# One core, the end of a fused layer: the last product is taken in another order, into one bank for each chunk of tokens

## The chip, the core and the metric

The kernel runs on one NeuronCore of a Trainium2 chip. The metric is device time in microseconds for one execution of the whole program. Engines are named as in the profile: PE is TensorE (PEld its weight loads), DVE is VectorE, ACT is ScalarE, POOL is GpSimd, SP is SyncE, which issues nearly all the DMAs here.

## The reference

Input `x` is 2 x 1024 tokens of 512 float32 values. It is normalised, goes through linear attention with 16 heads and, beside it, through a feed-forward block with routed low-rank experts; both results are added to `x`.

```python
xn = _layernorm(x)
# attention: Q, K after elu + 1; out = (Q @ KV) / (Q . K_sum) @ wo.T + bo
# feed-forward
gate = xn @ W_gate + _lora(xn, sA_gate, sB_gate) + _expert_lora(xn, A_gate, B_gate, w)
up   = xn @ W_up   + _lora(xn, sA_up, sB_up)     + _expert_lora(xn, A_up, B_up, w)
hidden = silu(gate) * up                                       # 1376 features
ffn = hidden @ W_down + _lora(hidden, sA_down, sB_down) + _expert_lora(hidden, A_down, B_down, w)
out = x + attention + ffn
```

Everything is float32. What the change touches is the last product alone: `hidden @ W_down`, the low-rank terms of the down projection and the attention's output product, which the kernel takes as one sum over features.

## The kernel before

**Stages.** Attention and the gate and up products come first and leave features in DRAM. The last stage, which begins after line 1590, reads the features back and multiplies them by the down weights. It works in four units `u` of 512 tokens (two groups of 256); `first_unit` does the first, `unit_of_two` the others. The last unit is `u == 3`; there `nxt` is false.

**Two levels of a fast product.** A unit's product is a 2 x 2 block product (two token groups by two halves of 256 output columns), taken with seven block products instead of eight. They are numbered `p`, and `A`, `B`, `C` and `E_` in `unit_of_two` gather them: `E_` takes `p = 3`, which is needed only in the block of group 0 and column half 1, and is the last of the unit. Each `p` is again a sum over feature blocks. For three pairs of feature blocks (`PAIRS`) the same seven-product scheme is used once more, inside the 256 tokens by 256 columns: two chunks of 128 tokens (`q` = 0, 1) by two column halves of 128 (`e` = 0, 1). These inner products are numbered `r`. The single feature block left over (`SINGLE`), the last features with the bias row (`hr`) and the low-rank term (`had`) are taken plainly, for each chunk over all 256 columns (`whole`).

**Two banks for each sum.** `X_AT` says that `r` = 1, 6, 5 and 7 lie side by side in one PSUM bank, named `px..`; these are shared by several of the four blocks of the output. `Y_AT` says that `r` = 2, 4 and 3 lie in a second bank, `py..`, each in the block it belongs to (order `(e q)`), and the plain terms are added onto the same second bank. `main` issues the products in the order 1, 2, 4, then the plain terms, then 5, 6, 7, 3.

**The way out.** `read` turns the shared bank into four blocks: ACT copies the first one (L1798), DVE makes running sums (L1799, L1800, L1801), adds them to the residual tile `xr` (L1809), then adds the second bank (L1811). In the last unit L1811 is done in two halves, one for each chunk `q`, with a store to DRAM after each (`halves=True`, `store_out` at L1617, its DMA at L1620). All matmuls of these sums are issued in `term`, so they have the line L1771; the bank's name (`pxe`, `pye` for `E_`) tells them apart. The low-rank terms are issued much earlier, by `low_rank_pair` right after the second product of the unit (L1995), so the bank `held2` of `E_` is begun there.

**Order.** The order of instructions on PE, DVE, ACT and POOL is the order in which the program writes them; each engine works through its own queue and waits for the others by semaphores. PSUM banks have tags: `E_` has `held1` and `held2`; `held3` holds `ph`, the low-rank sums, until `low_rank_weighted` (L1651) has read them.

Of the kernel before, what the change touches and what calls it, by code (L numbers as in the profile page):

```python
# [10 lines left out]
F32 = mybir.dt.float32  # L11
# [4 lines left out]
P = 128  # L16
# [21 lines left out]
def layer_kernel(  # L38
# [23 lines left out]
    nc = tc.nc  # L62
# [29 lines left out]
    NQ = UT // P  # L92
# [9 lines left out]
    def pool(stack, name, bufs=1, **k):  # L102
        return stack.enter_context(tc.tile_pool(name=name, bufs=bufs, reuse_waits="tile", **k))
# [91 lines left out]
    for b in range(NBATCH):  # L195
        t = p2.tile([P, 2, NC, 32], F32, name=f"ksd{b}")
# [41 lines left out]
    ps_pool = [pool(psum1, "ps1", space=PSUM)]  # L238
# [256 lines left out]
    class Finish:  # L495


        def __init__(self, b, pg, ksum):
            self.b, self.pg, self.ksum = b, pg, ksum
            self.made = 0  # L500
# [889 lines left out]
    B_OF = {1: 0, 2: 2, 3: 3, 4: 7, 5: 4, 6: 5, 7: 6}  # L1390
# [111 lines left out]
    feats = {}  # L1502
# [48 lines left out]
    for j in range(NP - 1):  # L1551
        if j > 0:
            load_weights(j + 1)
        first, second = next_pair(j + 1)
# [39 lines left out]
    H_OF = {1: 0, 2: 2, 3: 7, 4: 3, 5: 4, 6: 5, 7: 6}  # L1594
    ORDER = (1, 6, 5, 2, 7, 3, 4)
    d1, d2 = slice(0, HD), slice(HD, D)
    V, G = nc.vector, nc.gpsimd
# [10 lines left out]
    xq = {}  # L1608

    def load_out(u, g, h):  # L1610
        b, s = divmod(u, 2)
        first = b * BT + g * TB + s * UT
        t = p4w.tile([P, NQ, HD], F32, tag=f"xr{g}{h}", name=f"xr{u}_{g}{h}")
        nc.sync.dma_start(out=t, in_=x[first : first + UT, h * HD : (h + 1) * HD].rearrange("(q p) d -> p q d", p=P))
        xq[u, g, h] = t

    def store_out(u, g, h, q=slice(0, NQ)):  # L1617
        b, s = divmod(u, 2)
        first = b * BT + g * TB + s * UT
        nc.sync.dma_start(  # L1620
            out=out[first : first + UT, h * HD : (h + 1) * HD].rearrange("(q p) d -> p q d", p=P)[:, q, :],
            in_=xq[u, g, h][:, q, :],
        )

    def tmp(tag, name):
        return p4w.tile([P, D], F32, tag=tag, name=name, bufs=2 if tag == "w" else 1)
# [19 lines left out]
    def low_rank_weighted(u):  # L1646
        b, s = divmod(u, 2)
        had = p4w.tile([P, UT], F32, tag="had", name=f"had{u}")
        for g in range(2):
# [5 lines left out]
    LEFT = {2: (0, wdr[:, d1], bd_sb[:, d1]), 7: (1, wdr[:, d2], bd_sb[:, d2]),  # L1655
            3: (0, wdr[:, d2], bd_sb[:, d2]), 4: (1, wdr_diff, bd_diff)}

    def weights(n):
        return wd[n] if n < NP else kvo[n - NP]


    PAIRS = ((0, 1), (2, 3), (NP, NP + 1))
    SINGLE = NP - 1
    EH = HD // 2
# [5 lines left out]
    def t_at(k, i, sl):  # L1670

        if sl.start == 0:
            return weights(PAIRS[k][i // 2])[:, 1:2, (e0, e1)[i % 2]]
        return tw[k][:, i, sl.start - 2 : sl.stop - 2, :]
# [16 lines left out]
    def in_turn(*gs):  # L1691
        gs = list(gs)
        while gs:
            gs = [g for g in gs if next(g, gs) is not gs]

    def right(k, r, p):
        w0, w1 = (weights(n)[:, B_OF[p], :] for n in PAIRS[k])
        if r in (4, 5, 6):
            i = {5: 0, 6: 1, 4: 2}[r]
            return t_at(k, i, slice(B_OF[p], B_OF[p] + 1))[:, 0, :]  # L1700
        return {1: w0[:, e0], 2: w1[:, e0], 3: w1[:, e1], 7: w0[:, e1]}[r]
# [31 lines left out]
    def left_of(u, k, r, p):  # L1733
        f0, f1 = (feats[u, n][:, H_OF[p], :] for n in PAIRS[k])
        if r in (3, 5, 6, 7):
            i = next(i for i, ps in enumerate(BATCHES) if p in ps)
            j = sorted(BATCHES[i], key=H_OF.get).index(p)
            return si[u, i][k][:, {5: 0, 6: 1, 7: 2, 3: 3}[r], j, :]
        return {1: f0[:, 0:P], 2: f1[:, 0:P], 4: f1[:, P:UT]}[r]


    X_AT = {1: 0, 6: 1, 5: 2, 7: 3}
# [5 lines left out]
    class Out:  # L1748
# [12 lines left out]
        def term(self, out, lhsT, rhs, c):  # L1761
            v = (self.x, self.y)[c]
            first = v is None
            if first:
                v = self.bank(c)
                if c:
                    self.y = v
                else:
                    self.x = v
            o = v[:, out, :] if isinstance(out, int) else v.rearrange("p (e q) n -> p q e n", q=NQ)[:, out[0]]  # L1770
            nc.tensor.matmul(o, lhsT, rhs, start=first, stop=True, skip_group_check=True)  # L1771

        def whole(self, q, lhsT, rhs):

            self.term((q,), lhsT, rhs, 1)
# [15 lines left out]
                    self.whole(q, hr[:, g, ts(q, P)], w)  # L1791
            self.products(p, (5, 6, 7, 3))

        def read(self, *to, halves=False):

            w = tmp("w", f"w{self.name}_{self.made}").rearrange("p (c n) -> p c n", n=EH)
            self.made += 1
            nc.scalar.copy(w[:, 0], self.x[:, 0])  # L1798
            V.tensor_add(w[:, 1], w[:, 0], self.x[:, 1])  # L1799
            V.tensor_add(w[:, 2], w[:, 1], self.x[:, 2])  # L1800
            V.tensor_add(w[:, 1::2], w[:, 1:3], self.x[:, 3:4].to_broadcast([P, 2, EH]))  # L1801

            def by_block(t):
                return t.rearrange("p (e q) n -> p e q n", q=NQ)

            dst = [xq[self.u, g, h] for g, h in to]
            blocks = [t.rearrange("p q (e n) -> p e q n", n=EH) for t in dst]
            if len(dst) == 1:
                V.tensor_add(blocks[0], blocks[0], by_block(w))  # L1809
                for q in (slice(0, 1), slice(1, 2)) if halves else (slice(0, NQ),):  # L1810
                    V.tensor_add(blocks[0][:, :, q], blocks[0][:, :, q], by_block(self.y)[:, :, q])  # L1811
                    if halves:
                        store_out(self.u, *to[0], q)
            else:
                V.tensor_add(w, w, self.y)
                for v in blocks:
                    V.tensor_add(v, v, by_block(w))

    def low_rank_pair(had, first, second):

        for q in range(NQ):
            for p, o in (first, second):
                g, _, w = LEFT[p]
                rows = slice(g * ER, (g + 1) * ER)
                o.whole(q, had[rows, ts(q, P)], w[rows, :])

    def last_unit(u):
        return u == 3
# [15 lines left out]
    def S12(u, ns):  # L1844
        block_sum(u, 4, V.tensor_add, 1, 3, ns)
        block_sum(u, 5, V.tensor_sub, 4, 0, ns)
# [4 lines left out]
    def S4(u, ns):  # L1851
        block_sum(u, 7, V.tensor_sub, 2, 5, ns)
# [120 lines left out]
    def unit_of_two(u, hr, before):  # L1973
        nxt = not last_unit(u)
        turn = next_kvo() if u == 1 else None
        A, B, C, E_ = (
            Out(u, n, tx, ty)
            for n, tx, ty in (("a", "ab0", "ab1"), ("b", "x0", "x1"), ("c", "x0", "held0"), ("e", "held1", "held2"))
        )

        A.main(1)
        before()
        if turn:
            turn[0](slice(0, 2))
        S12(u, range(NF) if u > 1 else range(5, NF))
        low_rank_sums(u, hr, tuple(range(NP)))
        A.read((0, 0))
        had = low_rank_weighted(u)
        if nxt:
            hr_next = load_rest(u + 1)  # L1990
            load_blocks(u + 1, slice(0, 2))
        feature_pair_sums(u, 1)

        B.main(7, hr)
        low_rank_pair(had, (3, E_), (7, B))  # L1995
        if turn:
            turn[1]()
        B.read((1, 1))

        A.main(6)  # L2000
        S4(u, range(NF))
        feature_pair_sums(u, 2, (0,))
        A.read((1, 0))
        feature_pair_sums(u, 2, (1, 2))

        B.main(4, hr)
        low_rank_pair(had, (2, C), (4, B))
        if nxt:
            load_blocks(u + 1, slice(3, 4))
        if u == 2:  # L2010
            in_turn(weight_sums(2, slice(3, 4)))
        B.read((1, 0))
        store_out(u, 1, 0)
        if nxt:
            load_out(u + 1, 1, 0)

        A.main(5)
        feature_pair_sums(u, 3)
        if nxt:
            S3(u + 1, range(NF))  # L2020
        A.read((0, 1), (1, 1))
        store_out(u, 1, 1)
        if nxt:
            load_out(u + 1, 1, 1)
        if turn:
            turn[2]()

        C.main(2, hr)
        if nxt:
            load_blocks(u + 1, slice(2, 3))  # L2030
            feature_pair_sums(u + 1, 0)
        C.read((0, 0))
        store_out(u, 0, 0)
        if nxt:
            load_out(u + 1, 0, 0)
        if turn:
            turn[0](slice(2, 3))

        E_.main(3, hr)
        if turn:  # L2040
            turn[0](slice(3, 4))

        def after():
            E_.read((0, 1), halves=not nxt)
            if nxt:
                store_out(u, 0, 1)
                load_out(u + 1, 0, 1)
            if turn:
                turn[3]()

        if not nxt:
            after()
        return (hr_next, after) if nxt else None

    for g in range(2):
        for h in range(2):
# [65 lines left out]
```

## Time and profile before

| what | value |
|---|---|
| median of 3 runs | 729.91 us (728.38 to 730.34) |
| the profiled execution | 730.1 us |
| its span in the profile | 728.3 us |
| PE busy | 717.8 us (99%) |
| DVE busy | 579.8 us (80%) |
| the last unit's last product (`E_`) begins on PE | 716.42 us |
| the last matmul ends | 723.0 us |
| the last DVE add ends | 725.35 us |

Times in the trace count from the start of the span. The profiled execution's own time is 1.8 us longer than its span: what lies around the program. PE is busy from the first slice to the last but one, so the time is the work of PE, and then a tail in which PE has nothing to do. A busy entry of PE counts one issued pass; each float32 matmul here is two passes in the records, so three products of one `r` are six records.

### The profile page before, as it was taken

The page shows a single profiled execution, that of the slowest core. Times are in us where ns is not written, and L with a number is a line of the kernel's source. Part 1 is how long each engine was busy: PE and PEld are TensorE (multiplying, and loading weights), DVE is VectorE, ACT ScalarE, POOL GpSimd, SP SyncE. Part 2 cuts the span into 40 slices and gives each one's busy share as a digit, 9 for nine tenths or more (in the row PEclk, how much of TensorE's full clock was granted, in tenths as well). Part 3 has the DMA queues.
Part 4 walks back from the last instruction along what each step waited for, and adds up shares of the span by engine and source line. Part 5 has one row for each costly group of instructions (what it writes and reads, how often), then busy time and mean ns, then how long its engine had stood idle before and what let it go on. Part 6 is the DMA issues. An engine that isn't in the chain of part 4 may idle for free.

```text
span 728.3 us, 9908 instructions
## 1 busy us (share of the span) xinstructions
PE 717.8 (99%) x3428; PEld 493.1 (68%) x3428; DVE 579.8 (80%) x1330; ACT 198.1 (27%) x438; POOL 143.4 (20%) x176
## 2 busy tenths in 40 slices
PE   8999999999999999999999999999999999999997
PEld 6666676454433566666667667566688899899896
DVE  5788767777587588878878878878988789998874
ACT  3533412454443233333333333333200000000000
POOL 4014011101000770310310310544520100000000
PEclk9999999999999999999999999999999999999999
DMA  4253000313575101211201201333662444523101
GB/s 155 85 157 106 11 1 1 97 32 112 158 212 154 26 5 58 87 32 59 88 29 59 87 30 59 116 126 134 202 195 101 134 158 132 158 87 109 59 16 44
DMA packets 61734, 66.85 MB, mean 92 GB/s; under 512 B 10866, under 2 KB 49522, under 8 KB 61428
## 3 DMA queue, kind: packets, MB, share of 16 engines
q1 hardware_dynamic: 61154, 66.20, 29.0%
q8 instruction: 27, 0.44, 0.3%
q14 instruction: 23, 0.19, 0.1%
q10 hardware_dynamic: 530, 0.02, 0.0%
HBM read 44.11 MB, written 22.09 MB: 91 GB/s over the span
## 4 chain that ended last, share of the span: by engine, by line
PE 83%; DVE 12%; ACT 3%; issue 1%; DMA 0%; DVEq 0%; ACTq 0%
PE ab L1202 16%; PE b L1262 8%; PE po L1899 7%; PE pg L401 5%; PE pya L1771 4%; PE pxa L1771 3%; PE pqu L772 3%; PE pyb L1771 3%; PE ph L1639 3%; PE x L1202 3%; PE pxb L1771 2%; PE pyc L1771 2%; PE pxa L851 2%; PE b L1257 2%; PE pr L1090 2%; PE pye L1771 2%
## 5 line engine op out<-in xcount | busy, mean ns | idle before, releaser
L1262 PE MATMUL b<-t,w 128*128 128x512 f32 x160 | 83.2, 601 | 0.7 <-DVE t L1284 0.7
L401 PE MATMUL pg<-kt,xn 128*128 128x512 f32 x128 | 58.7, 594 | 0.5 <-DVE kt L345 0.5
L1284 POOL TENSOR_TENSOR r<-r,r 128x512 f32<-128x512 f32 x20 | 30.1, 1524 | 84.5 <-DVE t L1284 82.9
L1202 PE MATMUL ab<-ti,wi 128*128 128x256 f32 x180 | 45.4, 379 | 0.0
L1202 PEld LDWEIGHTS ab<-ti,w 128*128 128x128 f32 x140 | 25.1, 189 | 29.4 <-DVE r L1230 8.2
L1284 DVE TENSOR_TENSOR r<-r,r 128x512 f32<-128x512 f32 x60 | 44.9, 788 | 0.0
L1202 PEld LDWEIGHTS ab<-ti,wi 128*128 128x128 f32 x180 | 34.2, 190 | 13.2 <-issue 5.0
L1202 PE MATMUL ab<-ti,w 128*128 128x256 f32 x140 | 41.2, 387 | 0.5 <-DVE r L1230 0.2
L401 PEld LDWEIGHTS pg<-kt,xn 128*128 128x128 f32 x128 | 23.2, 190 | 22.6 <-issue 20.6
L1235 ACT COPY r<-ab 128x256 f32<-128x256 f32 x50 | 18.6, 372 | 71.1 <-PE ab L1202 71.1
L1230 DVE TENSOR_TENSOR r<-r,ab 128x256 f32<-128x256 f32 x50 | 20.8, 417 | 20.2 <-ACT r L1227 19.7
L1262 PEld LDWEIGHTS b<-t,w 128*128 128x128 f32 x160 | 29.2, 190 | 11.3 <-issue 5.9
L1238 DVE TENSOR_TENSOR r<-r,ab 128x256 f32<-128x256 f32 x50 | 20.8, 417 | 15.9 <-ACT r L1235 15.7
L1212 ACT COPY r<-ab 128x256 f32<-128x256 f32 x50 | 18.6, 373 | 48.5 <-PE ab L1202 47.0
L1899 PE MATMUL po<-wd,f 128*128 128x256 f32 x140 | 30.9, 380 | 0.1
L410 POOL TENSOR_TENSOR ksum<-ksum,kt 128x512 f32<-128x512 f32 x12 | 15.8, 1319 | 71.7 <-DVE lg L447 42.3
L1223 ACT COPY r<-ab 128x256 f32<-128x256 f32 x50 | 18.6, 372 | 40.8 <-PE ab L1202 40.8
L1899 PEld LDWEIGHTS po<-wd,f 128*128 128x128 f32 x140 | 26.4, 190 | 4.4 <-issue 0.5
L1202 PE MATMUL ab<-xnT,w 128*128 128x256 f32 x100 | 29.4, 390 | 0.0
L1842 DVE TENSOR_TENSOR f<-f 128x256 f32<-128x256 f32 x84 | 29.3, 416 | 0.1
L1202 PE MATMUL ab<-xnT,wi 128*128 128x256 f32 x100 | 28.1, 379 | 0.0
L1202 PEld LDWEIGHTS ab<-xnT,w 128*128 128x128 f32 x100 | 18.1, 189 | 10.8 <-issue 4.5
(450 smaller groups left out, 1655.7 us busy)
## 6 DMA issues: line engine op xcount, KB each, us to landing
h_dram<-h SPq DMA_DIRECT2D x40, 256.0 KB
f<-h_dram SPq DMA_DIRECT2D x10, 512.0 KB
x_ring<-in_x_dram SPq DMA_DIRECT2D x16, 256.0 KB
q_dram<-qt SPq DMA_DIRECT2D x16, 256.0 KB
xr<-in_x_dram SPq DMA_DIRECT2D x16, 256.0 KB
out_dram<-xr SPq DMA_DIRECT2D x15, 256.0 KB
w<-in_w_up_dram SPq DMA_DIRECT2D x10, 256.0 KB
w<-in_w_gate_dram SPq DMA_DIRECT2D x10, 256.0 KB
```

The source lines that it names most:

```text
L401: nc.tensor.matmul(pg[m], xns[n][:, ts(m, P)], kt, start=(j == 0), stop=(j == TPBATCH - 1))
L772: nc.tensor.matmul(banks[c], wqs[p][:, k, ts(c, P)], tsum[b][p][:, k, :], start=(start and k == 0), stop=(k == 1), skip_group_check=True,)
L1202: nc.tensor.matmul(out, w, t, start=start, stop=True, skip_group_check=True)
L1212: nc.scalar.copy(self.r[0][:, H0], self.ua)
L1230: nc.vector.tensor_add(self.r[1][:, H1], self.r[1][:, H1], self.lo)
L1238: nc.vector.tensor_add(self.r[1][:, H0], self.r[1][:, H0], self.lo)
L1262: nc.tensor.matmul(pb[m], ws[m][:, A_OF[p], ts(k, P)], tsum[b][p][:, k, :], start=start, stop=True, skip_group_check=True)
L1284: eng.tensor_add(to[m], t[m], v[m])
L1639: nc.tensor.matmul(phs[u][g * ER : (g + 1) * ER, :], a, f[:, g, :], start=(ns[0] == 0 and n == 0), stop=(last and n == len(chunks) - 1), s ...
L1771: nc.tensor.matmul(o, lhsT, rhs, start=first, stop=True, skip_group_check=True)
L1842: op(t[:, at, :], t[:, x_, :], t[:, y, :])
L1899: nc.tensor.matmul(ps[p][:, q, :], lhsT, rhs, start=start, stop=stop, skip_group_check=True)
```

## The change

The last unit's `E_` becomes an object of a new class, `LastOut`. It computes the same sum with the same matmuls, but:

- its `finish` issues the four shared products `r` = 1, 6, 5, 7 first, into a bank `pxz` (tag `held1`), and then the instructions that turn them into blocks and add these to `xr`;
- the second bank is split: chunk 0 has a bank `pyz0` (tag `held2`), chunk 1 a bank `pyz1` (tag `held3`);
- for each chunk in turn it issues that chunk's own products (`r` = 2 and 3 for chunk 0, `r` = 4 for chunk 1), its plain terms, an add of that bank to `xr` and a store of that chunk.

The low-rank terms still come from `low_rank_pair` at the same place, now into the two banks. Units 1 and 2 are as before; `read` loses its `halves` form.

```diff
+    class LastOut:
...
+        def term(self, q, e, lhsT, rhs):
+            first = self.ys[q] is None
+            if first:
+                self.ys[q] = ps_pool[0].tile([P, 2, EH], F32, tag=f"held{2 + q}", name=f"pyz{q}")
+            nc.tensor.matmul(self.ys[q][:, e], lhsT, rhs, start=first, stop=True, skip_group_check=True)
+
+        def finish(self, p, hr, to):
+            u, w_left = self.u, LEFT[p]
+            self.x = ps_pool[0].tile([P, 4, EH], F32, tag="held1", name="pxz")
+            for r in (1, 6, 5, 7):
+                for k in range(len(PAIRS)):
+                    nc.tensor.matmul(
+                        self.x[:, X_AT[r]], left_of(u, k, r, p), right(k, r, p), start=(r == 1 and k == 0), stop=True,
+                        skip_group_check=True,
+                    )
+            w = tmp("w", "wz").rearrange("p (c n) -> p c n", n=EH)
+            t = xq[u, to[0], to[1]]
+            nc.scalar.copy(w[:, 0], self.x[:, 0])
+            V.tensor_add(w[:, 1], w[:, 0], self.x[:, 1])
+            V.tensor_add(w[:, 2], w[:, 1], self.x[:, 2])
+            V.tensor_add(w[:, 1::2], w[:, 1:3], self.x[:, 3:4].to_broadcast([P, 2, EH]))
+            by_block = w.rearrange("p (e q) n -> p q e n", q=NQ)
+            blocks = t.rearrange("p q (e n) -> p q e n", n=EH)
+            V.tensor_add(blocks, blocks, by_block)
+            f = feats[u, SINGLE][:, H_OF[p], :]
+            for q in range(NQ):
+
+                for r, e in (((2, 0), (3, 1)), ((4, 0),))[q]:
+                    for k in range(len(PAIRS)):
+                        self.term(q, slice(e, e + 1), left_of(u, k, r, p), right(k, r, p))
+                self.whole(q, f[:, ts(q, P)], weights(SINGLE)[:, B_OF[p], :])
+                self.whole(q, hr[:, w_left[0], ts(q, P)], w_left[1])
+                V.tensor_add(blocks[:, q], blocks[:, q], self.ys[q])
+                store_out(u, *to, slice(q, q + 1))
...
+        if not nxt:
+            E_ = LastOut(u)
...
+        if not nxt:
+            E_.finish(3, hr, (0, 1))
+            return None
         E_.main(3, hr)
...
         def after():
-            E_.read((0, 1), halves=not nxt)
-            if nxt:
-                store_out(u, 0, 1)
-                load_out(u + 1, 0, 1)
+            E_.read((0, 1))
+            store_out(u, 0, 1)
+            load_out(u + 1, 0, 1)
```

More of the change, by code (lines that the diff above doesn't have):

```diff
@@ L1792, in main, with read @@
             self.products(p, (5, 6, 7, 3))
-        def read(self, *to, halves=False):
+        def read(self, *to):
             w = tmp("w", f"w{self.name}_{self.made}").rearrange("p (c n) -> p c n", n=EH)
@@ L1808, in read @@
             if len(dst) == 1:
[L1809 to L1813, printed above, removed]
+                for v in (w, self.y):
+                    V.tensor_add(blocks[0], blocks[0], by_block(v))
             else:
@@ L1817, in read, with __init__, whole @@
                     V.tensor_add(v, v, by_block(w))
+    class LastOut:
+        def __init__(self, u):
+            self.u = u
+            self.x = None
+            self.ys = [None] * NQ
+        def whole(self, q, lhsT, rhs):
+            self.term(q, slice(0, 2), lhsT, rhs)
+        def term(self, q, e, lhsT, rhs):
[30 more added lines that the diff above has]
+                store_out(u, *to, slice(q, q + 1))
     def low_rank_pair(had, first, second):
@@ L2043, in after @@
         def after():
-            E_.read((0, 1), halves=not nxt)
-            if nxt:
-                store_out(u, 0, 1)
-                load_out(u + 1, 0, 1)
+            E_.read((0, 1))
+            store_out(u, 0, 1)
+            load_out(u + 1, 0, 1)
             if turn:
                 turn[3]()
-        if not nxt:
-            after()
-        return (hr_next, after) if nxt else None
+        return hr_next, after
     for g in range(2):
```

## The prediction

> **What bounds the kernel now.** I read the page's busy times first, then the chain of waits over the last microseconds, then the order of instructions on PE and DVE there, then the DMA share in narrow windows.
>
> ```profile
> PE 717.8 (99%) x3428; PEld 493.1 (68%) x3428; DVE 579.8 (80%) x1330; ACT 198.1 (27%) x438; POOL 143.4 (20%) x176
> ```
>
> PE is never idle until its last matmul ends at about 723.0 us. So only two things can move the time: less work on PE, or a shorter tail behind it. The span is 728.3 us, so that tail is 5.3 us. The chain of waits from 722 us on says what it is made of (start, length, what):
>
> ```profile
> 722.00 0.35 PE pxe L1771 x3
> 722.35 0.03 ACTq L1798
> 722.37 0.04 issue
> 722.41 0.27 ACT we L1798
> ...
> 722.71 0.30 DVE we L1799
> ...
> 723.03 0.30 DVE we L1800
> ...
> 723.35 0.43 DVE we L1801
> ...
> 723.80 0.70 DVE xr L1809
> ...
> 724.60 0.42 DVE xr L1811
> 725.02 0.33 DVEq L2118
> ```
>
> The shared bank pxe is complete at 722.33, three matmuls of r = 3 before the end of PE. Then one copy and six adds run in a row, up to 725.35: 2.35 us after the last matmul. Of these, only the last two (L1811) need the other bank. When the shared bank is filled is a matter of order, as PE's own order of time shows:
>
> ```profile
> 716.42 0.61 PE L1771 MATMUL pxe<-wd,f 128*128 128x128 f32 x4
> ...
> 718.43 1.03 PE L1771 MATMUL pye<-wd,f 128*128 128x256 f32 x4
> 719.29 1.03 PE L1771 MATMUL pye<-wdr,hr 97*128 97x256 f32 x4
> ...
> 722.61 0.39 PE L1771 MATMUL pye<-kvo,si_3b 128*128 128x128 f32 x2
> ```
>
> The reader is to see that a third of the stage (717.09 to 720.16) fills pye between two parts of pxe. The rest of the tail, 725.35 to 728.3, is the last store and the end of the program. The windows there (stretch, then PE clock, DMA share and GB/s as the last three numbers):
>
> ```profile
> 725.50:725.80 0.30, 0.00 (x0) 0.00 (x0) 0.00 (x0) 0.00 (x0) 0.00 (x0) 1.00 0.00 0
> 725.80:726.00 0.20, 0.00 (x0) 0.00 (x0) 0.00 (x0) 0.00 (x0) 0.00 (x0) 1.00 0.43 143
> 726.60:726.80 0.20, 0.00 (x0) 0.00 (x0) 0.00 (x0) 0.00 (x0) 0.00 (x0) 0.88 0.93 312
> 727.20:728.30 1.10, 0.00 (x0) 0.00 (x0) 0.00 (x0) 0.00 (x0) 0.00 (x0) 0.50 0.00 0
> ```
>
> Two stores of 128 KB start to be issued on SP at 725.05 and about 725.45. Their bytes move from about 725.85 to 726.8, and SP's wait for them (1.31 us from 725.9) ends at 727.2. The last 1.1 us is the closing of the program on all engines.
>
> [...] The trace has about 1.75 us for the last store (725.45 to 727.2), which I use.
>
> **The change, step by step.**
>
> *PE's work.* The same matmuls in another order: 21 of 128 columns and 4 of 256, besides the low-rank ones. From the timeline, three products of one r take 0.67 us (716.42 to 717.09, 720.16 to 720.83), the plain terms 0.86 us for SINGLE and 0.87 for hr, both chunks, so 0.43 each per chunk. The sum is 7 x 0.67 + 4 x 0.43 = 6.41 us, as now. Changing between the two widths costs nothing in the trace (pitches stay at 0.67 across 718.43 and 720.16). PE's end stays at 723.0. I price PE at nothing, with -0.1 to +0.3 us for the new order of banks, which the trace does not show.
>
> *The shared bank comes first.* Four r from 716.42 take 2.68 us. The last pair of records begins 0.23 us before that and lasts 0.39: complete at 719.26. The copy begins 0.08 us later, as now (722.33 to 722.41), so at 719.34. From there to the end of L1809 is 2.08 us now (722.41 to 724.49), so the blocks are in xr at 721.42. Is DVE free? Product C is read out there: its last add begins at 718.18 and lasts 0.69, so DVE is idle from 718.87 and ACT long before. This whole 2.08 us then lies beside PE's work, which goes on until 723.0: 1.58 us of cover is left. Does DVE's read of one bank slow PE's writes to another? In C's read-out it does the same (pxc read from 715.99 to 717.35 while PE fills pxe and pye), at an unchanged 0.67 us per r.
>
> *What the moved products need.* r = 6, 5, 7 are issued from 717.09 instead of 719.95. Their left sides (si) are done on DVE at 708.1, so the margin falls from 11.9 to 9.0 us: nothing. The bank held1 was last used in the unit before.
>
> *Chunk 0.* From 719.10 PE does r = 2 and 3 and two plain terms: 2 x 0.67 + 2 x 0.43 = 2.20 us, to 721.30, complete 0.16 us later (720.16 against 720.32 for such a group now): 721.46. DVE has just finished (721.42); it waits for PE and adds at about 721.54 to 721.96. SP issues the store from 722.0 to 722.4. Behind this wait on DVE's queue stands only chunk 1's add, on SP's queue only chunk 1's store, and neither could start earlier.
>
> *Chunk 1.* From 721.30: 0.67 + 2 x 0.43 = 1.53 us, to 722.83, complete at 723.0. The add begins 0.08 us later and takes 0.42: DVE ends at **723.50** instead of 725.35: **-1.85 us**. What is left behind PE is one wait and one add.
>
> *Stores.* Still two of 128 KB. Chunk 0's bytes move at about 722.85 to 723.3, before chunk 1's store is issued at 723.55; now the second issue stands behind the first one's (725.05 plus 0.37) and starts about 0.1 us after its add instead of 0.05. That is -0.05 us, with -0.3 (the last store alone on the queues, a shorter wait for its end) to +0.1 as bounds. The part from the last issue to the end, 2.85 us, stays.
>
> *The low-rank terms.* Chunk 1's now begin held3 at about 690.4, instead of the other half of held2. ph in held3 has been read when the second L1651 ends, at 684.4, and had, which the same matmul needs, comes from that instruction. No wait is new: margin 6 us. Instruction counts on every engine are equal.
>
> *Sum.* -1.85 - 0.05 = **-1.9 us**, with -2.3 to -1.5 from the bounds. Against the profiled execution: a span of 726.4 and a time of 730.1 - 1.9 = 728.2. That execution lies 0.2 us above the median of the runs, so for the median 729.91 - 1.9 = **728.0 us**, or 0.26%.
>
> **The rivals.**
>
> *As worked out, -1.9 us* (0.75). The bound of what this kernel's measurement can tell from no change is about 0.3%, 2.2 us; so the likeliest gain lies just inside it. The three runs of before spread over 1.96 us; a median taken again may fall 0.7 us to either side. So 0.45 of this case would read as over 0.3% faster.
>
> *The last store gains more, -2.2 to -2.5 us* (0.12). For it: it is alone, and the wait after its last byte (726.8 to 727.2) may shrink. Against it: C's 256 KB store, also alone, takes the same 0.85 us from issue to its first bytes, and the two last ones barely overlap now. Time about 727.6.
>
> *The wait of chunk 0's add is tied to a later matmul* (0.08). If it is released only with PE's end, both adds run from 723.08 to 723.83 and both stores follow each other as now: -1.5 us, 728.4. Against it: the banks are separate tiles, and pxe's reader is already released at 722.33, before PE's last three matmuls.
>
> *TensorE loses its pace in the new order: slower* (0.03). Between 719.3 and 722 PE would write pyz0 and pyz1 while ACT and DVE read pxz, and 128- and 256-column passes alternate more often. The gain is gone once PE's stage of 6.4 us takes 1.9 us more, and the run is measurably slower from 4.1 us, 64% more: passes of 0.11 us would have to become 0.18. At 5 us lost the time is 733. C's read-out speaks against it.
>
> *The change does nothing* (0.02): if the copy at the head of the chain still waited for PE's end, the chain would run as now, 729.9. The order on each engine is the written one, so I see no way.
>
> **How the numbers follow.** Faster by over 0.3%: 0.45 x 0.75 + 0.6 x 0.12 + 0.2 x 0.08, about 0.43. Slower: 0.03. Within: 0.54. The range: -2.3 to -1.5 us with 0.7 us of the median's own scatter on both sides gives 726.9 to 729.1, and the lower end takes in the second case. I keep that.
>
> **What would show it.** In the changed profile: PE's order pxz x24 from 716.4 to 719.1, then pyz0, then pyz1, with PE's end still at 723.0. The copy starts near 719.35, the add of the blocks ends near 721.4, the add of chunk 0 at 721.5, that of chunk 1 at 723.1 to 723.5. The chain ends PE pyz1, one DVE add. Two separate bursts of DMA, near 723 and 724.6. The span is 726.4. I am wrong if PE's stage is longer than 6.5 us, if the last add begins more than 0.2 us after PE's end, or if more than 3.0 us lie between DVE's end and the span's.

## The result, and the profile after

| | before | changed |
|---|---|---|
| median of 18 runs each | 729.94 us (726.82 to 730.58) | 726.57 us (724.57 to 728.42) |
| ratio, with its 95% interval | 1 | 0.9973 (0.9963 to 0.9983) |
| profiled execution: time, span | 730.1, 728.3 us | 724.7, 722.9 us |
| the last product begins on PE | 716.42 us | 713.15 us |
| from there to PE's end | 6.58 us | 6.59 us |
| from there to the end of the last DVE add | 8.93 us | 7.05 us |
| from there to the end of the span | 11.89 us | 9.79 us |

The ratio says 0.27% less, 2.0 us. The two medians differ by 3.4 us and the two profiled spans by 5.4 us. These are not three effects of the change. The table shows that in the profiled execution the last product already begins 3.3 us sooner, at a place in the program that the change has not reached. The stage that was changed is 2.1 us shorter. The experiments keep the two apart: from here on, times called *counted from the last product* are taken from its first matmul.

The chain of waits of the changed kernel, from 713 us on (start, length, what):

```profile
713.31 2.68 PE pxz L1838 x24
715.99 3.76 PE pyz L1831 x26
719.75 0.02 issue
719.78 0.42 DVE xr L1859
```

Where the chain of before ended in a copy and six adds behind PE, PE's own work now reaches to 719.75 and one add follows. The instructions of DVE and ACT beside it, in order of time (start, length, engine, line, operation, and in brackets the idle time before it):

```profile
716.08 0.27 ACT L1844 COPY wz<-pxz 128x128 f32<-128x128 f32 x1 [3.08 <-PE pxz L1838]
...
716.37 0.29 DVE L1845 TENSOR_TENSOR wz<-wz,pxz 128x128 f32<-128x128 f32 x1 [0.77 <-ACT wz L1844]
...
717.47 0.69 DVE L1850 TENSOR_TENSOR xr<-xr,wz 128x512 f32<-128x512 f32 x1
...
718.27 0.42 DVE L1859 TENSOR_TENSOR xr<-xr,pyz 128x256 f32<-128x256 f32 x1
...
719.78 0.42 DVE L1859 TENSOR_TENSOR xr<-xr,pyz 128x256 f32<-128x256 f32 x1 [1.09 <-PE pyz L1831]
```

The copy waits for pxz, not for PE's end: it begins at 716.08, and PE goes on to 719.75. The shared blocks are in xr at 718.16, chunk 0 is added at 718.27, and then DVE itself waits 1.09 us for PE. That last wait is the mark of a tail that has been emptied: DVE is now early. The windows of the last store (the last two numbers are the DMA share and GB/s):

```profile
721.00:721.20 0.20, 0.00 (x0) 0.00 (x0) 0.00 (x0) 0.00 (x0) 0.00 (x0) 1.00 0.52 174
721.20:721.40 0.20, 0.00 (x0) 0.00 (x0) 0.00 (x0) 0.00 (x0) 0.00 (x0) 1.00 1.05 358
721.40:721.60 0.20, 0.00 (x0) 0.00 (x0) 0.00 (x0) 0.00 (x0) 0.00 (x0) 1.00 0.39 123
721.60:723.00 1.40, 0.00 (x0) 0.00 (x0) 0.00 (x0) 0.00 (x0) 0.00 (x0) 0.83 0.00 0
```

One burst of 128 KB stands alone, where before two ran into each other for 0.95 us. The last bytes move about 1.35 us after the last add ends (720.20), against 1.45 before.

### The profile page after: what moved, and what is told of

The parts are those of the page before. It is cut to its first block, busy times and chain, and to the rows that moved or that the text cites. A ratio compares the mean times of both kernels' runs of the same rounds, so it can differ in the third digit from the quotient of the medians.

```text
span 722.9 us, 9907 instructions
## 1 busy us (share of the span) xinstructions
PE 714.9 (99%) x3428; PEld 491.3 (68%) x3428; DVE 579.9 (80%) x1330; ACT 198.2 (27%) x438; POOL 143.7 (20%) x176
## 4 chain that ended last, share of the span: by engine, by line
PE 83%; DVE 13%; ACT 3%; issue 1%; DMA 0%; DVEq 0%
PE ab L1202 16%; PE b L1262 8%; PE po L1942 7%; PE pg L401 5%; PE pya L1771 4%; PE pxa L1771 3%; PE pqu L772 3%; PE pyb L1771 3%; PE ph L1639 3%; PE x L1202 3%; PE pxb L1771 2%; PE pyc L1771 2%; PE pxa L851 2%; PE b L1257 2%; PE pr L1090 2%; PE kua L430 2%
```

## The experiments

Two theories stand against each other: the *order* theory (the tail is what must follow the bank that is filled last, so taking the shared products first is what counts) and the *banks* theory (a bank, an add and a store for each chunk bring the gain). A third question is where the 3.3 us ahead of the last product come from.

**The changed kernel again (e1_again).** No edit.

> The changed kernel once more, unaltered. Times are counted from the first matmul of the last product. Theory (the tail is shortened by the order of the products; the rest of the difference between the two profiled executions is scatter in the first 20 us): PE ends at 6.6, the last DVE add at 7.05, the span at 9.75 (each within 0.1), wherever the last product begins (713 or 716 us from the span's start). Rival (the change also makes the stages before it 3.3 us faster): the last product begins at 713 again.

The last product begins at 713.16, PE ends at 6.59, DVE at 7.04, the span at 9.79, counted from the last product. So the stage repeats. That it began at 713 again was what the rival named, and this run alone does not refute it. Two later ones do: e5, which turned out to be the same program in effect, began its last product at 714.88, and e10, the kernel before with only its start altered, at 713.11. The 18 runs gave 0.9979 (0.9969 to 0.9989), from 724.77 to 728.45 us.

**The order alone (e2_order_alone).** The shared products stay first; the chunks share one bank again, with both adds and stores at the end.

```diff
             if first:
-                self.ys[q] = ps_pool[0].tile([P, 2, EH], F32, tag=f"held{2 + q}", name=f"pyz{q}")
...
+                self.y = ps_pool[0].tile([P, NQ, 2, EH], F32, tag="held2", name="pyz")
...
-                V.tensor_add(blocks[:, q], blocks[:, q], self.ys[q])
+            for q in range(NQ):
+                V.tensor_add(blocks[:, q], blocks[:, q], self.y[:, q])
                 store_out(u, *to, slice(q, q + 1))
```

> Shared products first, but one bank for both chunks' own sums, both adds and both stores after the last matmul. Counted from the last product's first matmul. Theory (what counts is how much work waits for the bank that is filled last): PE ends at 6.6, then 0.08 of wait and both adds, 0.75: DVE ends at 7.4, the span at 10.3 with the stores close behind each other, so 1.5 us less than before. Rival (a bank, an add and a store for each chunk bring the gain): DVE ends at 8.9 and the span at 11.9, as before.

DVE's order of time at the end (PE's last matmul ends at 719.82, the last product began at 713.23):

```profile
719.86 0.75 DVE L1860 TENSOR_TENSOR xr<-xr,pyz 128x256 f32<-128x256 f32 x2 [1.62 <-PE pyz L1831]
```

Both adds now wait for PE, 1.62 us. DVE ends at 7.38 and the span at 10.34: 1.55 us of the 2.10 come from the order. That chunk 0 can be added before PE's end only from a bank of its own is not shown: no run adds it early out of a shared one. The five runs gave 0.9955 (0.9940 to 0.9970), better than the changed kernel itself. The stage cannot do that. It is a matter of the start of the program, of which more below: the runs of a kernel fall into three groups by it, and none of these five (725.36 to 727.20 us) lies in the slowest.

**The banks alone (e3_banks_alone).** A bank, an add and a store for each chunk, and the products in the old order.

```diff
...
+            shared((1,))
+            own(0, 2, 0)
+            own(1, 4, 0)
+            for q in range(NQ):
+                self.whole(q, f[:, ts(q, P)], weights(SINGLE)[:, B_OF[p], :])
+            for q in range(NQ):
+                self.whole(q, hr[:, w_left[0], ts(q, P)], w_left[1])
+            shared((6, 5, 7))
+            own(0, 3, 1)
...
```

> A bank, an add and a store for each chunk, but the products in the old order, with the shared sum complete three matmuls before the end. Counted from the last product's first matmul. Theory: as before, DVE ends at 8.9 and the span at 11.9, because the shared chain of 2.08 us still comes first and both own sums are complete long before it ends. Rival (the banks bring the gain): DVE ends at 7.1, the span at 9.8.

```profile
720.55 0.69 DVE L1866 TENSOR_TENSOR xr<-xr,wz 128x512 f32<-128x512 f32 x1
721.35 0.75 DVE L1868 TENSOR_TENSOR xr<-xr,pyz 128x256 f32<-128x256 f32 x2
```

The last product began at 713.17: DVE ends at 8.93 and the span at 11.89, the numbers of before to 0.01 us. The banks theory falls. It also speaks against a change in the stages ahead: this kernel has the changed banks and begins its last product at 713, and yet its 20 runs lie between 726.57 and 730.59 us, as those of before do (726.49 to 730.64; ratio 0.9989, 0.9978 to 0.9999).

**The shared products last (e4_shared_last).** Each chunk has its bank, add and store; its own products come first.

> Each chunk has its bank, add and store, but its own products come first and the shared products last. Counted from the last product's first matmul. Theory: the shared bank is complete at 6.6, the whole chain lies behind it: 0.08 + 2.08 + 0.11 + 0.75, DVE ends at 9.6 and the span at 12.5, 0.7 us more than before. Rival (the banks bring the gain, or any order does): at most 8.9 and 11.9.

The chain of waits at the end (PE's last matmul ends at 723.2, the last product began at 716.60):

```profile
723.26 0.27 ACT wz L1851
...
724.66 0.70 DVE xr L1857
...
725.38 0.42 DVE xr L1859
725.80 0.33 DVEq L2163
```

DVE ends at 9.53 and the span at 12.4, 0.6 and 0.5 us later than before (0.7 was expected of both; the gap ahead of the last two adds is 0.02 instead of 0.09 us, and what closes it is not shown). The same banks thus make the end faster or slower, by the order alone. The 12 runs' ratio, 1.0001 (0.9986 to 1.0016), does not show it.

**Both stores at the end (e5_stores_together).** The two stores were written after chunk 1's add.

> The changed kernel, but chunk 0's store is held back: both stores are issued after chunk 1's add. Counted from the last product's first matmul, DVE ends at 7.05 as in the changed kernel. Theory (a last store that stands alone ends the program 0.2 us sooner after its add): both stores are issued one behind the other at 7.1 and 7.5, later still than before by 0.35 us, so from DVE's end to the span's end it takes 3.1 to 3.3 us instead of 2.7 to 2.8. Rival (that part varies from execution to execution): 2.7 to 3.0 us.

The edit did not do what it was for. SP's row shows the first of the two issues at 720.45, right after chunk 0's add ended at 720.42: here SP waited for the data of the store, not for chunk 1's add, which is written ahead of it and begins at 721.50. DVE ends at 7.04 and the span at 9.79; it is in effect one more execution of the changed kernel, and the theory about the last store is not tested by it. It began its last product at 714.88.

**A longer shared chain (e6_chain_plus_2).**

```diff
...
+            spare = tmp("r", "spare").rearrange("p (c n) -> p c n", n=EH)
+            for _ in range(2):
+                V.tensor_add(spare, w, w)
             V.tensor_add(blocks, blocks, by_block)
```

> The changed kernel with two more DVE adds of 512 columns (0.69 us each, into a spare tile that nothing reads) in the shared chain, ahead of its add to xr. Counted from the last product's first matmul, the chain now ends at 5.0 and chunk 1's bank is readable at 6.6. Theory (the chain lies beside PE's work, with 1.1 us of cover besides chunk 0's add): of 1.42 us added about 0.2 to 0.3 shows: chunk 0's add begins at 6.45 instead of 5.1, DVE ends at 7.25. Rival (the chain is still on the path, or TensorE waits for it): DVE ends at 8.4 to 8.5.

```profile
719.12 1.42 DVE L1852 TENSOR_TENSOR spare<-wz 128x512 f32<-128x512 f32 x2
720.45 0.68 DVE L1853 TENSOR_TENSOR xr<-xr,wz 128x512 f32<-128x512 f32 x1
721.24 0.75 DVE L1862 TENSOR_TENSOR xr<-xr,pyz 128x256 f32<-128x256 f32 x2
```

The last product began at 714.80. Chunk 0's add begins at 6.44 and DVE ends at 7.19: of 1.42 us of work, 0.14 show. DVE no longer waits for PE at all, so the cover is used up; that further work in the chain would be paid is an estimate from this. The two stores stand close here, and from DVE's end to the span's end it takes 2.90 us instead of 2.75.

**One store (e9_one_store).** `store_out(u, *to)` once, after both adds.

> The changed kernel with one store of 256 KB after chunk 1's add in place of two of 128 KB. Counted from the last product's first matmul, DVE ends at 7.05 as in the changed kernel. Theory (what follows the last add is the last store's bytes and a fixed part): 256 KB move in 0.85 instead of 0.45 us, so from DVE's end to the span's end it takes 3.1 to 3.2 us, the span ends at 10.2. Rival (bytes don't count, only the number of stores that are close together): 2.7 to 2.8, the span at 9.8.

The last product began at 713.02, DVE ends at 7.05 (720.07), the span at 10.2 (723.2). From DVE's end to the span's end it is 3.10 us, 0.36 more than in the changed kernel. So the bytes of the last store are paid. If the first 128 KB cost as much as these further 128 KB did, the other 2.4 us don't depend on the bytes; that is an estimate from these two traces. Over all executions, one last store of 128 KB that stands alone has 2.74 to 2.75 us there (the changed kernel, e1, e5, e8), two close ones 2.90 to 2.96 (before, e2, e3, e4, e6, e10).

SP's own instructions say where the difference lies. The issues of the last two stores, in before and in the changed kernel (count, then shortest, median and longest in ns, then the starts of the first and the last):

```profile
L1620 SPq DMA_DIRECT2D out_dram<-xr x2: 345/384/424, 725.0 to 725.4; - x2
L1620 SPq DMA_DIRECT2D out_dram<-xr x2: 344/344/344, 718.7 to 720.2; - x2
```

In before the last issue stands behind the first: it begins 0.09 us after the last add and takes 0.42 us. In the changed kernel it begins 0.03 us after the add and takes 0.34. That is 0.15 us of the 0.22. The wait for the store is 0.03 us shorter (1.28 instead of 1.31), and what follows that wait 0.06 (0.98 instead of 1.04). The last part does not hang on the distance of the stores, since e4 and e6, with close ones, also have 0.98; why it varies is open.

**Chunk 1 cut once more (e7_three_parts).** Its second column half gets its own bank, add of 128 columns and store of 64 KB.

```diff
...
+            own(1, 4, 0)
+            for e in range(2):
+                for l, m in plain:
+                    self.term(1 + e, slice(0, 1), l[:, ts(1, P)], m[:, (e0, e1)[e]])
+                V.tensor_add(blocks[:, 1, e], blocks[:, 1, e], self.ys[1 + e][:, 0])
+                store_out(u, *to, slice(1, 2), (e0, e1)[e])
```

> The changed kernel with chunk 1 cut once more: its second column half has a third bank, an add of 128 columns and a store of 64 KB; the plain terms of chunk 1 become two matmuls of 128 columns each. Counted from the last product's first matmul. Theory (behind PE's end stands only what needs the last bank): PE ends at 6.6 to 6.7, the last add takes 0.29 instead of 0.42, DVE ends at 6.95, and 64 KB move in 0.2 us less than 128 KB: the span ends at 9.4 to 9.5, 0.3 us before the changed kernel. Rival (the fixed part of a store and of the closing decides, and three issues stand closer on SP): 9.7 to 9.9, no gain. In the runs' ratio to the changed kernel neither can be told.

```profile
721.74 0.29 DVE L1872 TENSOR_TENSOR xr<-xr,pyz 128x128 f32<-128x128 f32 x1 [0.16 <-PE pyz L1835]
```

Begun at 715.09, PE ends at 6.62, DVE at 6.94, the span at 9.61. The add's 0.1 us is gained; of the store's 0.2 us, 0.08 is. The last 64 KB, in rows of 512 bytes instead of 1 KB, reach 251 GB/s in a window of 0.2 us, where the 128 KB reached 358; that the shorter rows are the reason is not shown. The gain is 0.18 us instead of 0.3, and the runs (0.9974, 0.9963 to 0.9984) don't show it.

**The start of the program (e8_warm_24, e10_before_warm_24, e11_warm_24_three_parts).** PE's order of time at the start, in the profiled execution of before,

```profile
1.37 4.10 PE L249 MATMUL warm<-ident 128*128 128x128 f32 x18 [1.37 <-POOL ident masks.py:199]
6.51 1.08 PE L308 MATMUL pt<-ident,xn 128*128 128x128 f32 x4 [1.04 <-DVE xn L298]
7.52 2.07 PE L676 MATMUL pbk<-bk_sb,ones 1*128 1x512 f32 x2
9.52 4.78 PE L362 MATMUL pk<-wk_sb,xnT 128*128 128x256 f32 x12
```

and in that of the changed kernel:

```profile
6.15 0.67 PE L308 MATMUL pt<-ident,xn 128*128 128x128 f32 x4 [0.67 <-DVE xn L298]
6.75 1.12 PE L676 MATMUL pbk<-bk_sb,ones 1*128 1x512 f32 x2
7.80 2.90 PE L362 MATMUL pk<-wk_sb,xnT 128*128 128x256 f32 x12
```

(pt holds transposes of x, pbk a bias row spread over 128 rows, pk a product with the key weights.) The instructions are the same; pbk and pk take 2.07 and 4.78 us in one, 1.12 and 2.90 us in the other. In before, one pass of pk follows the other after 0.43 to 0.44 us until 13.4 us; after that, and in the changed kernel from its first pk on, after 0.22. In before, PE does its first real work at half pace. The 18 dummies (`warm`) have half pace in both kernels: they begin 0.21 us apart (the first two 0.27), as the four passes of pt do in before (0.21 to 0.24), where those of the changed kernel begin 0.11 to 0.15 us apart. The dummies end at about 5.5 us in both, and PE is then idle until its first real work. The traces also record the granted clock. The stretches of full or half clock in this record last 3.413, 713.386 or 716.799 us (leaving out the one in which the program ends), which are 1, 209 and 210 times 3.413.

The record begins with a stretch of full clock, at 5.71 us in the changed kernel and at 13.37 in before; this beginning is called the release here. Ahead of it the views print 1.00, so the row of granted clock on the profile page reads 9 throughout in both, and the half pace can be read from the passes alone. In three runs (e5, e6, e7) the record itself shows half a clock. PE in e5 in three stretches that follow each other (the last three numbers are granted clock, DMA share and GB/s):

```profile
4.92:8.33 3.41, 2.22 (x10) 1.00 1.05 364
8.33:11.75 3.42, 3.42 (x9) 0.50 0.39 95
11.75:15.16 3.41, 3.41 (x19) 1.00 0.40 97
```

In the first stretch lie the end of the dummies and the idle time; PE worked 2.22 of its 3.41 us. In the next one the granted clock is 0.50, and pk takes 4.58 us instead of 2.90.

By the moment of the release the ten traces with 18 dummies fall into three groups. With a release at 5.6 to 6.2 us the last product begins at 713.0 to 713.2 (the changed kernel, e1, e2, e3, e9). With one at 4.6 to 5.2 the clock is halved once more for 3.41 us, and the last product begins at 714.8 to 715.1 (e5, e6, e7). With one at 13.4 or 13.6 it begins at 716.4 or 716.6 (before, e4). What sets the moment of the release is not shown: in before PE is busy without a pause from 6.51 us on, 2 us of it with pbk, whose operands have a single row, and the release comes at 13.37.

e8 and e10 raise `WARM` from 18 to 24, in the changed kernel and in before, e11 in the three-part one.

> The changed kernel with 24 instead of 18 dummy transposes at the start of PE, which fill its idle time from 5.05 us to about 6.3. Its end is as in the changed kernel (9.75 from the last product's first matmul). Theory (the executions differ by up to 3.3 us because PE does its first work, from 6.2 to about 12 us, at full or at half pace, and at half pace when it fell idle between 5.1 and 6.5): the first real matmuls are never at half pace for long, the last product begins at 713 in nearly every run and the runs above 727.5 us vanish: median 725 to 726, ratio to before 0.995 to 0.996. Rival (the differences come from when the first loads land): the runs spread from 724.6 to 728.4 as before, ratio 0.9975, or 0.2 us worse for the transposes that stand ahead of the first real work.

> The kernel before with 24 instead of 18 dummy transposes at the start and nothing else changed. Theory (the dummies take away the scatter of the first 15 us, the change shortens the end by 2.1 us): runs within about 1 us of each other, median 726.8 to 727.0, which is 2.0 to 2.2 us above the changed kernel with the same dummies (724.79); DVE ends at 8.9 and the span at 11.9 from the last product's first matmul. Rival (part of the changed kernel's gain comes from elsewhere): a difference under 1.5 or over 2.6 us.

> The changed kernel with 24 dummies and chunk 1 in two column halves, each with a bank, an add and a store. Theory: 0.1 to 0.2 us under the changed kernel with 24 dummies, 724.6 to 724.7 us, at the edge of what its runs can tell; the span ends 9.6 from the last product's first matmul. Rival (nothing gained by the further cut): 724.8 or more.

The start of e8:

```profile
1.37 5.15 PE L249 MATMUL warm<-ident 128*128 128x128 f32 x24 [1.37 <-POOL ident masks.py:199]
6.58 0.66 PE L308 MATMUL pt<-ident,xn 128*128 128x128 f32 x4
7.16 1.12 PE L676 MATMUL pbk<-bk_sb,ones 1*128 1x512 f32 x2
```

There is no long idle time ahead of pt, and pbk takes 1.12 us; the release is at 6.14 us, in e10 at 5.76. The six runs of e8 lie between 724.70 and 725.89 us, median 724.79; the five of e10 between 726.69 and 727.24, median 726.81. With so little scatter the change is worth 726.81 - 724.79 = **2.02 us**, and the stages say the same: counted from the last product, the span ends at 9.79 in e8 and at 11.89 in e10. (The two were run on different chips; the runs of before on both lie around 728.5 and 730.1 us.) Against before, e8 has the ratio 0.9944 (0.9928 to 0.9961), e10 0.9965 (0.9951 to 0.9978). So the dummies bring about as much as the change (0.35 and 0.27%, with intervals that overlap), and both together have the lowest ratio here.

e11 missed: its median is 726.15 us (724.54 to 726.28), not 724.6. Its end is as expected (9.61 from the last product), but that began at 714.69 instead of 713.49. PE's release came late, at 7.19 us, and its first pk begins 0.40 us later than in e8. Then PE waits 0.43 us for DVE (L298, which makes the normalised x) ahead of the second pt; that DVE row takes 1.50 us there and 0.83 in e8. The traces show a pattern in this row: in all 13 of them it ends either 0.55 us after its own start or 0.28 us after the end of the POOL instruction (L326 to L329) that was running when it began, whichever is later, to 0.02 us. In e11 it began 0.04 us after such an instruction of 1.26 us did. No experiment tests this, and of e11's four slower runs (726.09 to 726.28 us) only one has a trace.

## Why the prediction was right

- *Bound and place.* PE's work is unchanged (6.59 against 6.58 us), and the whole gain of the stage lies in the tail behind it. Confirmed. (That "a third of the stage" filled pye between the two parts of pxe was misread: 717.09 to 720.16 is 3.07 of 6.58 us, nearly half. No term rests on it.)
- *The shared chain.* Counted from the last product: the copy predicted at 2.92, found at 2.93; the blocks in xr at 5.00, found 5.01; chunk 0's add at 5.12, found 5.12; DVE's end at 7.08, found 7.05. The cover of 1.58 us was there: with chunk 0's add (0.42) and its gap taken from it, about 1.1 us are left, in which DVE waits for PE; e6 used them up. Absolute times came out 3.3 us sooner than the text has them, because its profile of before had the late release.
- *The wait tied to a later matmul* (1.5 us) and *the loss of pace* (slower) did not occur: the copy and chunk 0's add were released while PE went on, at an unchanged 0.67 us per r.
- *The stores* are the term that was mis-sized: -0.05 us was taken, with -0.3 as the bound. The part from DVE's end to the span's end fell from 2.96 to 2.75 us in all four executions of the changed ending, so -0.2. The text counted only that the last issue would start sooner after its add (0.07 us). It let the part from that issue to the end stay at 2.85 us; that fell by 0.15, because the issue itself was 0.08 us shorter, the wait 0.03 and the closing 0.06. With it, -1.88 - 0.22 gives -2.1 by the stages, between the main case and the rival *the last store gains more* (-2.2 to -2.5).
- *Size.* 1.9 us predicted, 2.0 measured by the ratio: within the 0.3% that this measurement resolves, as forecast. That the ratio comes so near to the stages owes something to luck: both kernels happened to have similar shares of runs with an early and a late release, where e2 shows a better ratio for a smaller gain in the stage.
- *The median is not the 728.0 of the text* but 726.57, 0.3 us below the range of 726.9 to 729.1, and the sum is not the reason. "A median taken again may fall 0.7 us to either side" took three runs of before for the whole spread; the same changed kernel had a median of 726.57 in its first 18 runs and of 727.98 in e1. The runs of both kernels fall into three groups. Of 46 runs of before (beside e1), they lie around 727.0, 728.4 and 730.1 us, 7, 16 and 23 of them; of 36 of the changed kernel, around 724.8, 726.4 and 728.1, 5, 10 and 21. The groups' middles differ by 2.25, 2.03 and 2.06 us. A median depends on which group holds the middle run: for the first 18 it fell into the uppermost group for before, into the middle one for the changed kernel. The traces tie each group to a moment of PE's release. For the middle group each run shows it as well: the mean granted clock is 0.998 in all 10 runs of the changed kernel, where the 5 of the lowest group have 0.999 or 1.000, and 3.41 us at half a clock in 725 are 0.0024. For the uppermost group two traces show the late release; five of its 44 runs have a mean clock of 0.995, by that figure an estimated 6 to 7 us at half a clock, and that the others are like the two traces is argued.

## What to carry to other kernels

At the end of a program, ask of each instruction behind the last matmul whether it needs the bank that is filled last; what doesn't should have its matmuls first, and only then is it worth splitting the rest by bank, add and store. Order gave 1.55 of 2.10 us here, the split the last 0.55, and the split without the order nothing. Price such a change in its own stage, from its first instruction to the end of the span, because a median of runs that fall into groups can move by much of the effect: here by 1.4 us between two sets of 18 runs of one kernel.

## What was not expected of the hardware

- The first real matmuls run at half or at full pace from execution to execution (pbk 2.07 or 1.12 us), and this makes up to 3.3 us of 730. In e5 the clock was halved for 3.41 us after a stretch as long in which PE had been idle for 1.2 us and worked for the other 2.22. Six more dummy transposes closed the idle time ahead of the first real work. Both kernels then had little scatter (1.2 us in the six runs of e8, where 36 had 3.9), but e11 shows that the start can still come 1.2 us later for another reason.
- Two stores of 128 KB that are issued one right behind the other cost about 0.15 us more at the end of the program than two that stand apart, all of it on SP (the last issue starts 0.07 us later and takes 0.42 instead of 0.34 us). 128 KB more in the last store cost 0.36 us (one trace, e9).
